# A two-layer graph network on one core: edges and stored products in transfers for two spans, one table for x1 and x1 @ W1m, degrees summed in layer 1, and four slots in the ring

## The chip, the cores and the metric

The kernel runs on 1 core of one Trainium2 chip. The metric is the device time of one execution in microseconds (us), and a version's time is the median of its runs. All engines (TensorE, VectorE, ScalarE, GpSimd, and SyncE, which here only issues transfers) work from instruction queues of their own. In the profile they are called PE (with PEld for its weight loads), DVE, ACT, POOL and SP.

## The reference

There are N = 6250 nodes with D = 256 features, and E = 106250 edges, sorted by their target `dst`, with 256 features each. Everything is float32. Both layers gather a row for each edge's source, and sum over the edges of each target:

```python
# layer 0
msg = relu(x[src] + edge_attr)
h   = 2 * x + segment_sum(msg, dst)
f   = gelu(bn1(h) @ W1.T + b1) @ W2.T + b2
x1  = layernorm(x + bn2(h + f))
# layer 1
m   = gelu((x1[src] + edge_attr) @ W1m + b1m) @ W2m + b2m
agg = segment_sum(m, dst) / maximum(deg, 1)          # deg: edges per target
u   = gelu(agg @ W1u + b1u) @ W2u + b2u
x2  = layernorm(x1 + layernorm(x1 + u))
```

The layer norms have no scale of their own except the inner one of layer 1.

## The kernel before

**Tiles, spans, blocks.** The edges lie in 831 tiles of 128. Eight tiles make a span (V = 104 spans), in two groups of four. The nodes lie in 25 blocks of 256 (the last has 106). Since the edges are sorted by target, the targets of a span fall in a short window of nodes.

**The ring.** The gathered rows of a span stand in one of `RING` = 5 buffers, `rings[v % RING]`. `gather` (L793) issues eight indirect DMAs on POOL for a span, each of 128 rows of 1 KB, and before the first of them POOL waits until span v - 5 has been read out of that buffer.

**Layer 0, a loop over spans** (`step_0`). In step v: SP loads the edges of span v + 3 (`load_edges`, L776, 1 MB); POOL gathers for v; PE transposes the edges of v's first group (`turned`, L806; ACT copies to eaT, L811) and multiplies them by W1m (`product`, L819), DVE copies that to the tile z (L1101, L1110), and SP stores z into `zst` (L1111, 512 KB), so that layer 1 need not multiply the first group again. For span v - 1 ACT copies the edges into PSUM (`lifted`, L830) and DVE adds them to the gathered rows (`add_to_gathered`, L837); ACT applies relu (`activated`, L845). For span v - 2 PE sums the rows into 128 slots by one-hot matrices (L854 makes them on DVE; `into_slots`, L876), and ACT copies the slots out of PSUM (`kept_slots`, L885). For span v - 3 PE sums the slots into the accumulators of the blocks (`into_blocks`, L904). The ring's rows have a column of ones behind the 256 features, so with a width of 257 the slots hold their number of edges as well; a further matmul (L912) and additions on DVE (L917) make the degree of each node, on one partition.

**Blocks of layer 0.** When a block has all of its edges, the generator `nodes_0` goes through its dense part, a stage in each step: it stores the degrees (L974, 1 KB), computes x1 and stores it to `x1d` (L1018), then y = x1 @ W1m + b1m, and stores that to `proj` (L1042).

**Layer 1** (`step_1`) has the same steps. It gathers from `proj`, takes the first group's product from `zst` (L1249, 512 KB), loads the second group's edges (L776, 512 KB) and multiplies them, and applies gelu. For each new block SP loads x1 (L1242) and the degrees, spread over all partitions (L1244). At the end of a step `invert()` (L1266 to L1268) computes max(deg, 1), its reciprocal, and min(deg, 1). `nodes_1` begins with the product of the sums and the reciprocal (L1174) and ends with the store of the output (L1233). The first gather of layer 1 waits for the last store into `proj`.

**Order.** All of this stands in `tc.manual_schedule()`: each engine's instructions run in the order in which the program writes them. In that order SP's loads for span v + 3 come at the beginning of step v, and the stages of the blocks come once in the middle of a step (`advance(early)`) and once at its end (`advance(late)`). `end_0` and `end_1` write out the last spans of a layer, and `finish` the stages that are left.

## Time and profile before

| what | us |
|---|---|
| median of 3 runs (2175.54 to 2177.23) | 2176.7 |
| the profiled execution | 2862.04 |
| its span | 2860.2 |
| busy in it: PE | 2061.7 |
| busy in it: POOL | 1577.4 |
| busy in it: DVE | 1404.1 |
| busy in it: ACT | 1344.0 |

The profile is of one execution, and that one took nearly a third longer than the runs of the median. Durations of single instructions are to be taken from it with that in mind, and its waits even more so. A row of a group gives its line, engine, operation, the tiles that it writes and reads, and the number of instructions; behind the bar stand its busy time, the mean of one in ns, the idle time of the engine just before them, and what ended most of that.

### The profile page before, as it was taken

The numbers are of one execution on the slowest core, as the hardware profiler recorded it, in microseconds if no ns is written. First come the engines' busy times: TensorE is split into PE (matmuls) and PEld (weight loads), VectorE is DVE, ScalarE is ACT, GpSimd is POOL, SyncE is SP. The second block draws the span as 40 slices with busy tenths as digits, with TensorE's granted clock in tenths as the row PEclk, the third lists the DMA queues.
The fourth block names the chain that finished last, engine by engine and source line by source line (L and its number), as shares of the span: only waits on it lengthen the run. The fifth ranks groups of instructions, "written<-read, shape, count | busy, mean of one in ns | idle before, by whom it ended". The sixth has DMA issues, their size and how long they took to land.

```text
span 2860.2 us, 37166 instructions
## 1 busy us (share of the span) xinstructions
PE 2061.7 (72%) x11784; PEld 1524.6 (53%) x11784; DVE 1404.1 (49%) x4130; ACT 1344.0 (47%) x2138; POOL 1577.4 (55%) x1671
## 2 busy tenths in 40 slices
PE   3688788878788788788357757766776666665876
PEld 2465556556566555556245545544555555554654
DVE  3455555455455555555134534454454445454545
ACT  1355555455555555555133534444444444443544
POOL 5566566565565566662555554555555554555550
PEclk7789999899899999999678888897888888887988
DMA  6667676676677676674545544554555554554540
GB/s 213 202 221 229 216 239 222 209 239 218 214 231 228 212 246 223 220 241 133 168 152 164 171 155 148 176 170 150 167 174 172 164 166 148 164 174 146 183 154 14
DMA packets 312069, 531.71 MB, mean 186 GB/s; under 512 B 36325, under 2 KB 231480, under 8 KB 311736
## 3 DMA queue, kind: packets, MB, share of 16 engines
q1 hardware_dynamic: 231416, 309.65, 32.2%
q0 software_dynamic: 79744, 217.71, 24.9%
q8 instruction: 97, 1.59, 0.2%
q10 hardware_dynamic: 704, 1.87, 0.2%
q14 instruction: 108, 0.88, 0.1%
HBM read 455.34 MB, written 73.75 MB: 185 GB/s over the span
## 4 chain that ended last, share of the span: by engine, by line
PE 22%; another core or an unknown queue 13%; DVE 6%; issue 5%; ACT 5%; DMA 1%; POOL 1%; ACTq 0%; DVEq 0%; POOLq 0%
PE workP L819 10%; PE acc L904 3%; PE slotP L876 3%; PE nodeP L1211 2%; PE workP L806 2%; DVE ring L837 1%; PE nodeP L1184 1%; DMA ring<-proj,src_sb 1%; DVE hot L854 1%; ACT L961 1%; ACT ring L845 1%; ACT workP L830 1%; ACT eaT L811 1%; DVE uT L1189 1%
## 5 line engine op out<-in xcount | busy, mean ns | idle before, releaser
L793 POOL DMA_INDIRECT ring<-proj,src_sb x831 | 788.1, 948 | 683.9 <-issue 362.3
L793 POOL DMA_INDIRECT ring<-in_x_dram,src_sb x831 | 787.5, 948 | 525.9 <-issue 246.3
L819 PE MATMUL workP<-w1m_sb,eaT 128*128 128x256 f32 x3324 | 910.1, 419 | 159.7 <-ACT eaT L811 113.0
L819 PEld LDWEIGHTS workP<-w1m_sb,eaT 128*128 128x128 f32 x3324 | 662.9, 208 | 369.0 <-ACT eaT L811 118.5
L837 DVE TENSOR_TENSOR ring<-workP,ring 128x512 f32<-128x512 f32 x832 | 542.2, 682 | 626.9 <-remote 381.5
L904 PE MATMUL acc<-hot,sums 128*128 128x160 f32 (+19 forms) x1360 | 264.2, 331 | 304.9 <-DVE hot L898 176.1
L845 ACT ACTIVATE ring<-ring 128x1024 f32<-128x1024 f32 x418 | 441.8, 1058 | 65.6 <-DVE ring L837 46.0
L830 ACT COPY workP<-ea 128x512 f32<-128x512 f32 x624 | 345.4, 596 | 121.2 <-DVE ring L837 76.2
L904 PEld LDWEIGHTS acc<-hot,sums 128*128 128x128 f32 x1360 | 209.6, 216 | 343.8 <-DVE hot L898 131.4
L885 ACT COPY sums<-slotP 128x257 f32<-128x257 f32 (+1 forms) x208 | 77.0, 370 | 631.6 <-remote 314.7
L811 ACT COPY eaT<-workP 128x512 f32<-128x512 f32 x416 | 227.0, 586 | 306.7 <-PE workP L806 179.3
L876 PE MATMUL slotP<-ring,hot 128*32 128x257 f32 (+1 forms) x3324 | 277.0, 416 | 121.5 <-remote 64.4
L806 PE MATMUL workP<-ident,ea 128*128 128x128 f32 x1662 | 252.1, 289 | 147.2 <-DVE z L1101 75.3
L806 PEld LDWEIGHTS workP<-ident,ea 128*128 128x128 f32 x1662 | 201.9, 148 | 213.6 <-DVE z L1101 97.0
L854 DVE TENSOR_SCALAR hot<-ramp,slot 128x32 f32<-128x32 f32 x1662 | 265.5, 257 | 0.0
L876 PEld LDWEIGHTS slotP<-ring,hot 128*32 128x32 f32 x3324 | 112.4, 115 | 251.5 <-issue 110.3
L1194 ACT ACTIVATE uT<-uT,cols_sb 128x256 f32<-128x256 f32 (+1 forms) x100 | 44.6, 495 | 257.6 <-DVE uT L1189 221.4
L917 DVE TENSOR_TENSOR degs<-degs,slotP 1x160 f32<-1x160 f32 (+24 forms) x170 | 36.3, 241 | 253.7 <-remote 104.8
L1101 DVE COPY z<-workP 128x512 f32<-128x512 f32 x104 | 71.1, 684 | 172.9 <-remote 104.7
L1184 PE MATMUL nodeP<-fT,w 128*128 128x256 f32 x368 | 92.8, 394 | 17.2 <-issue 16.1
L1110 DVE COPY z<-workP 128x512 f32<-128x512 f32 x104 | 71.3, 686 | 39.7 <-PE workP L819 26.2
L961 ACT ACT_TABLE_LOAD x70 | 89.8, 1283 | 1.2
(138 smaller groups left out, 1469.1 us busy)
## 6 DMA issues: line engine op xcount, KB each, us to landing
ea<-in_edge_attr_dram SPq DMA_DIRECT2D x103, 1024.0 KB
zst<-z SPq DMA_DIRECT2D x104, 512.0 KB
ea<-zst SPq DMA_DIRECT2D x104, 512.0 KB
ea<-in_edge_attr_dram SPq DMA_DIRECT2D x103, 512.0 KB
ring<-in_x_dram,src_sb POOLq DMA_INDIRECT x831
ring<-proj,src_sb POOLq DMA_INDIRECT x831
xb<-in_x_dram SPq DMA_DIRECT2D x24, 256.0 KB
x1d<-x SPq DMA_DIRECT2D x24, 256.0 KB
```

Of the source, the lines that this page charges most:

```text
L793: nc.gpsimd.indirect_dma_start(out=rings[v % RING][:n, g * G + j, :D], out_offset=None, in_=table, in_offset=bass.IndirectOffsetOnAxis(ap= ...
L806: nc.tensor.transpose(pe[:, j, k, :n], ea[:n, q + j, k * P : (k + 1) * P], ident[:n, :n])
L811: nc.scalar.copy(eaT[:, j:k, :, :n], pe[:, j:k, :, :n])
L819: nc.tensor.matmul(ph[:n, j, :], lhsT=eaT[:, j, k, :n], rhs=w1m_sb[:, k, :], start=(k == 0), stop=(k == KC - 1),)
L830: nc.scalar.copy(ps[:n, j:k, :], of[:n, q + j : q + k, :])
L837: nc.vector.tensor_add(r[:n, at + j : at + k, :D], ps[:n, j:k, :], r[:n, at + j : at + k, :D])
L845: nc.scalar.activation(at, at, func)
L854: nc.vector.tensor_scalar(hots[v][:n, j, :], ramp[:n, :SLOTS], slot[:n, t : t + 1], None, op0=ALU.is_equal,)
L876: nc.tensor.matmul(ps[q * SLOTS : (q + 1) * SLOTS, :width], lhsT=hot[:n, j, :], rhs=r[:n, j, :width], start=(i == 0), stop=(i == PAIR - 1 ...
L904: nc.tensor.matmul(acc[b][:, k, cols], lhsT=its[:, k * P : (k + 1) * P], rhs=at, start=(begins and k == 0), stop=(last_span[b] == v and k ...
L961: nc.scalar.activation(mv[:n, :H, 1], mv[:n, :H, 1], AF.Sqrt, bias=eps[:n, :])
L1184: nc.tensor.matmul(ps[:, o - i, :width], lhsT=w12[:, k, o * P : (o + 1) * P], rhs=mT[:, k, :width], start=(k == 0), stop=(k == KC - 1),)
```

## The change

The edges are loaded into tiles for two spans (three buffers of 16 KB per partition): 2 MB in one transfer in layer 0, and in layer 1 1 MB from `zst` and twice 512 KB of edges. z is one tile for two spans, in one buffer, and is stored once in two steps. x1 and y are written into one tile and stored together into `table`, [N, 2, 256]; layer 1 gathers rows of 1 KB from it with doubled indices (`twice_src`, made once on DVE), and loads x1 from every second row. The degrees are no longer summed in layer 0: layer 1 takes the slots with a width of 257, ACT spreads their counts over 128 columns (`counts`), and the matmul and the additions then give the degree of each node on all partitions. What `invert()` did stands at the beginning of `nodes_1`. The ring has four buffers. The diff, without the last spans' lines and renamed tiles of the setup:

```diff
 SPAN = P // SLOTS * PAIR
-RING = 5
+RING = 4
 ROW = 260
...
     dram = ctx.enter_context(tc.tile_pool(name="dram", bufs=1, space=bass.MemoryType.DRAM))
-    proj = dram.tile([N, D], F32, name="proj")
-    x1d = dram.tile([N, D], F32, name="x1d")
-    degd = dram.tile([1, N], F32, name="degd")
-    zst = dram.tile([len(window), P, G * D], F32, name="zst")
+    table = dram.tile([N, 2, D], F32, name="table")
+    x1d = table[:, 1, :]
+    pairs_of_spans = -(-len(window) // 2)
+    zst = dram.tile([pairs_of_spans, P, 2 * G * D], F32, name="zst")
...
         tc.tile_pool(name="state", bufs=1) as state,
-        tc.tile_pool(name="edges", bufs=AHEAD + 1) as ep,
+        tc.tile_pool(name="edges", bufs=3) as ep,
         tc.tile_pool(name="hots", bufs=2) as hp,
...
+        twice_src = check.tile([P, T], I32, name="twice_src")
+        def rows_of_table():
+            nc.vector.tensor_scalar(twice_src, src_sb, 2.0, None, op0=ALU.mult)
         def norms():
...
-        def load_edges(v, some, to):
-            counts = sum((tiles_of(v, g) for g in some), [])
+        eas = {}
+        def load_rows(to, t0, tiles):
+            counts = [min(P, E - t * P) for t in range(t0, min(T, t0 + tiles))]
             for j, k, n in runs(counts):
-                r0 = (v * SPAN + some[0] * G + j) * P
+                r0 = (t0 + j) * P
                 nc.sync.dma_start(
...
-        def edge_tiles(v):
-            ea = ep.tile([P, SPAN, D], F32, name="ea")
-            for g in range(GROUPS):
-                eas[v, g] = ea[:, g * G : (g + 1) * G, :]
-            return ea
-        def gather(v, table):
+        def edges_0(i, pieces=1):
+            if i >= pairs_of_spans:
+                return
+            ea = ep.tile([P, 2 * SPAN, D], F32, name="ea")
+            for h in range(2 * GROUPS):
+                eas[2 * i + h // GROUPS, h % GROUPS] = ea[:, h * G : (h + 1) * G, :]
+            m = 2 * SPAN // pieces
+            for h in range(0, 2 * SPAN, m):
+                load_rows(ea[:, h : h + m, :], 2 * i * SPAN + h, m)
+        def edges_1(i):
+            if i >= pairs_of_spans:
+                return
+            ea = ep.tile([P, 2 * SPAN, D], F32, name="ea")
+            spans = [v for v in (2 * i, 2 * i + 1) if v < V]
+            for h, v in enumerate(spans):
+                eas[v, 0] = ea[:, h * G : (h + 1) * G, :]
+                eas[v, 1] = ea[:, (h + GROUPS) * G : (h + GROUPS + 1) * G, :]
+            m = len(spans) * G
+            nc.sync.dma_start(
+                out=ea[:, :m, :].rearrange("p j d -> p (j d)"), in_=zst[i][:, : m * D]
+            )
+            for v in spans:
+                load_rows(eas[v, 1], v * SPAN + G, G)
+        def gather(v, of, rows):
             for g in range(GROUPS):
...
                         out_offset=None,
-                        in_=table,
-                        in_offset=bass.IndirectOffsetOnAxis(ap=src_sb[:n, t : t + 1], axis=0),
+                        in_=of,
+                        in_offset=bass.IndirectOffsetOnAxis(ap=rows[:n, t : t + 1], axis=0),
                     )
...
-        hots, hot2s, sums = {}, {}, {}
+        hots, hot2s, sums, counts = {}, {}, {}, {}
...
                     )
-            sums[v] = hp.tile([P, D + 1], F32, name="sums"), ps
+            sums[v] = hp.tile([P, D], F32, name="sums"), ps
             return ps[:, :width]
...
         def kept_slots(v, ps):
-            nc.scalar.copy(sums[v][0][:, : ps.shape[-1]], ps)
+            nc.scalar.copy(sums[v][0], ps[:, :D])
+            if ps.shape[-1] > D:
+                counts[v] = hp.tile([P, P], F32, name="counts")
+                nc.scalar.copy(counts[v], ps[:, D : D + 1].to_broadcast([P, P]))
...
             (its, ps), hot, lo0 = sums.pop(v), hot2s.pop(v), window[v][0]
-            rest = ps[:1, D + 1 :]
+            rest = ps[:, D + 1 :]
             for b, lo, hi in parts(v):
...
                 nc.tensor.matmul(
-                    rest[:, :span], lhsT=its[:, D : D + 1], rhs=hot[:, :span], start=True, stop=True
+                    rest[:, :span], lhsT=counts.pop(v), rhs=hot[:, :span], start=True, stop=True
                 )
...
-        def nodes_0(b, acc, xb, deg):
+        def nodes_0(b, acc, xb):
             width, H, n = shape(b)
-            nc.sync.dma_start(out=degd[:, b * SB : b * SB + width], in_=deg[:, :width])
             fT = npool.tile([P, KC, SB], F32, name="fT")
...
                 )
-            hT = npool.tile([P, KC, SB], F32, name="hT", bufs=3)
+            hT = npool.tile([P, KC, SB], F32, name="hT")
             nc.vector.tensor_copy(hT[:, :, :width], acc[:, :, :width])
...
             ps = node_work()
-            gT = npool.tile([P, KC, SB], F32, name="gT")
+            gT = npool.tile([P, 2 * KC, SB], F32, name="uT")
             for o in range(KC):
...
             nc.vector.tensor_add(ps, ps, xb[:n, :H, :])
-            x1 = npool.tile([P, SH, D], F32, name="x1")
+            both = npool.tile([P, SH, 2, D], F32, name="both", bufs=3)
+            y, x1 = both[:, :, 0, :], both[:, :, 1, :]
             nc.vector.tensor_add(x1[:n, :H, :], ps, bn2_b[:n, None, :].to_broadcast([n, H, D]))
...
             scaled(x1, x1, mv, n, H)
-            nc.sync.dma_start(out=rows_of(x1d, b), in_=x1[:n, :H, :])
             yield
...
             yield
-            y = npool.tile([P, SH, D], F32, name="y", bufs=3)
             ps = node_work()
...
             )
-            nc.sync.dma_start(out=rows_of(proj, b), in_=y[:n, :H, :])
-        eas, xbs, acc, degs = {}, {}, {}, {}
+            nc.sync.dma_start(
+                out=rows_of(table.rearrange("n a d -> n (a d)"), b),
+                in_=both[:n, :H].rearrange("p h a d -> p h (a d)"),
+            )
+        xbs, acc, zs = {}, {}, {}
         def load_0(v):
-            load_edges(v, range(GROUPS), edge_tiles(v))
             for b in range(blocks):
...
                     )
-            degs[b] = npool.tile([1, SB], F32, name="degs", bufs=4)
-            nc.vector.memset(degs[b], 0.0)
             return False
...
         def full_0(v):
-            for b in into_blocks(v, acc, opened_0, degs):
-                begun(b, nodes_0(b, acc.pop(b), xbs.pop(b), degs.pop(b)))
-        zs = {}
+            for b in into_blocks(v, acc, opened_0):
+                begun(b, nodes_0(b, acc.pop(b), xbs.pop(b)))
...
             if v < V:
-                gather(v, x)
+                gather(v, x, src_sb)
                 first = turned(v, 0, 0, eas[v, 0])
                 second = turned(v, 0, 2, eas[v, 0])
-                zs[v] = ep.tile([P, G, D], F32, name="z", bufs=2)
+                if v % 2 == 0:
+                    zs[v // 2] = ep.tile([P, 2, G, D], F32, name="z", bufs=1)
             if 0 <= u < V:
...
             if v < V:
-                nc.vector.tensor_copy(zs[v][:, 0:2, :], product(*first))
+                nc.vector.tensor_copy(zs[v // 2][:, v % 2, 0:2, :], product(*first))
             if 0 <= u < V:
...
                 activated(u, 0, AF.Relu)
+            if v % 2 == 0:
+                edges_0(v // 2 + 2)
             if 0 <= w < V:
                 slot_nodes(w)
-                kept_slots(w, into_slots(w, D + 1))
+                kept_slots(w, into_slots(w, D))
             if v < V:
-                nc.vector.tensor_copy(zs[v][:, 2:4, :], product(*second))
-                nc.sync.dma_start(out=zst[v], in_=zs.pop(v).rearrange("p j d -> p (j d)"))
+                nc.vector.tensor_copy(zs[v // 2][:, v % 2, 2:4, :], product(*second))
+                if v % 2 or v == V - 1:
+                    z, m = zs.pop(v // 2), v % 2 + 1
+                    nc.sync.dma_start(
+                        out=zst[v // 2][:, : m * G * D],
+                        in_=z[:, :m].rearrange("p s j d -> p (s j d)"),
+                    )
             advance(late)
...
             slot_nodes(u - 1)
-            kept_slots(u - 1, into_slots(u - 1, D + 1))
+            kept_slots(u - 1, into_slots(u - 1, D))
             advance(under_way)
...
             slot_nodes(u)
-            kept_slots(u, into_slots(u, D + 1))
+            kept_slots(u, into_slots(u, D))
             full_0(u)
...
                 load_1(v)
+            for i in range(2):
+                edges_1(i)
             finish()
...
-        def nodes_1(b, acc, x1, deg, inv):
+        def nodes_1(b, acc, x1, deg):
             width, H, n = shape(b)
+            inv = npool.tile([P, SB], F32, name="inv", bufs=1)
+            nc.vector.tensor_scalar(inv[:, :width], deg[:, :width], 1.0, None, op0=ALU.max)
+            nc.vector.reciprocal(inv[:, :width], inv[:, :width])
+            nc.vector.tensor_scalar(deg[:, :width], deg[:, :width], 1.0, None, op0=ALU.min)
             mT = npool.tile([P, KC, SB], F32, name="fT")
...
             yield
-            uT = npool.tile([P, UC, SB], F32, name="uT")
+            uT = npool.tile([P, max(UC, 2 * KC), SB], F32, name="uT")
             for i in range(0, UC, 2):
...
             nc.scalar.copy(ps[:n, :H, :], x1[:n, :H, :])
-            r = npool.tile([P, SH, D], F32, name="hT", bufs=3)
-            y = npool.tile([P, SH, D], F32, name="y", bufs=3)
+            both = npool.tile([P, SH, 2, D], F32, name="both", bufs=3)
+            r, y = both[:, :, 0, :], both[:, :, 1, :]
             for to, name in ((r, "L1_gnn_b2u"), (y, "L1_gnn_beta")):
...
-        x1s, degs_1, acc_1, invs = {}, {}, {}, {}
+        x1s, degs_1, acc_1 = {}, {}, {}
...
                     nc.sync.dma_start(out=x1s[b][:n, :H, :], in_=rows_of(x1d, b))
-                    degs_1[b] = npool.tile([P, SB], F32, name="degb", bufs=4)
-                    nc.sync.dma_start(
-                        out=degs_1[b][:, :width],
-                        in_=degd[:, b * SB : b * SB + width].to_broadcast([P, width]),
-                    )
-            edge_tiles(v)
-            nc.sync.dma_start(out=eas[v, 0].rearrange("p j d -> p (j d)"), in_=zst[v])
-            load_edges(v, [1], eas[v, 1])
...
             acc_1[b] = psa.tile([P, KC, SB], F32, name="acc")
-            fresh.append(b)
+            degs_1[b] = npool.tile([P, SB], F32, name="degs", bufs=4)
+            nc.vector.memset(degs_1[b], 0.0)
             return True
-        fresh = []
-        def invert():
-            while fresh:
-                b = fresh.pop()
-                width, deg = shape(b)[0], degs_1[b]
-                invs[b] = npool.tile([P, SB], F32, name="inv")
-                inv = invs[b][:, :width]
-                nc.vector.tensor_scalar(inv, deg[:, :width], 1.0, None, op0=ALU.max)
-                nc.vector.reciprocal(inv, inv)
-                nc.vector.tensor_scalar(deg[:, :width], deg[:, :width], 1.0, None, op0=ALU.min)
         def full_1(v):
-            for b in into_blocks(v, acc_1, opened_1):
-                begun(b, nodes_1(b, acc_1.pop(b), x1s.pop(b), degs_1.pop(b), invs.pop(b)))
+            for b in into_blocks(v, acc_1, opened_1, degs_1):
+                begun(b, nodes_1(b, acc_1.pop(b), x1s.pop(b), degs_1.pop(b)))
...
             if v < V:
-                gather(v, proj)
+                gather(v, table.rearrange("n a d -> (n a) d"), twice_src)
             some = 0 <= u < V
...
                 slot_nodes(w)
-                kept_slots(w, into_slots(w, D))
+                kept_slots(w, into_slots(w, D + 1))
+            if v % 2 == 0:
+                edges_1(v // 2 + 2)
             if some:
...
             advance(late)
-            invert()
...
         begin()
+        edges_0(0, pieces=2)
+        edges_0(1)
         for v in range(AHEAD):
             load_0(v)
...
-        beside = {1: norms, 2: weights_of_layer_1, 3: strays, 6: join_weights}
+        beside = {1: norms, 2: weights_of_layer_1, 3: strays, 4: rows_of_table, 6: join_weights}
```

More of the change, by code (lines that the diff above doesn't have):

```diff
@@ L657, in node_work @@
             return work() if draining else psn.tile([P, 2, D], F32, name="nodeP")
-        dst_sb = check.tile([P, T], I32)
+        dst_sb = check.tile([P, T], I32, name="edge")
         tiles_i = check.tile([P, T], I32)
@@ L724, in strays @@
         def strays():
-            off = check.tile([P, T], F32)
+            off = check.tile([P, T], F32, name="edge")
             nc.vector.tensor_copy(off, tiles_i)
@@ L1310, in end_1 @@
             full_1(u - 2)
-            invert()
             activated(u - 1, 1, AF.Gelu)
@@ L1316, in end_1 @@
             slot_nodes(u - 1)
-            kept_slots(u - 1, into_slots(u - 1, D))
+            kept_slots(u - 1, into_slots(u - 1, D + 1))
             advance(under_way)
@@ L1325, in end_1 @@
             slot_nodes(u)
-            kept_slots(u, into_slots(u, D))
+            kept_slots(u, into_slots(u, D + 1))
             full_1(u)
```

## The prediction

> **What bounds the kernel now.** I read the page first, then POOL's waits, then a stretch of the timeline in which POOL waits for nothing, then the chain of waits around the change of layers.
>
> ```profile
> span 2860.2 us, 37166 instructions
> PE 2061.7 (72%) x11784; PEld 1524.6 (53%) x11784; DVE 1404.1 (49%) x4130; ACT 1344.0 (47%) x2138; POOL 1577.4 (55%) x1671
> ...
> L793 POOL DMA_INDIRECT ring<-proj,src_sb x831 | 788.1, 948 | 683.9 <-issue 362.3
> L793 POOL DMA_INDIRECT ring<-in_x_dram,src_sb x831 | 787.5, 948 | 525.9 <-issue 246.3
> L819 PE MATMUL workP<-w1m_sb,eaT 128*128 128x256 f32 x3324 | 910.1, 419 | 159.7 <-ACT eaT L811 113.0
> ```
>
> The profiled execution took 2862.0 us (span 2860.2 and 1.8 around it), 685 us more than the median of 2176.7. Its shares of busy time are therefore not those of a timed run; what is wanted is the engine that would set 2176.7. The timeline shows the pace of the gathers when nothing holds them:
>
> ```profile
> 1379.09 0.98 POOL L793 DMA_INDIRECT ring<-proj,src_sb  x1 [63.28 <-DMA proj<-y]
> 1380.38 0.95 POOL L793 DMA_INDIRECT ring<-proj,src_sb  x1 [0.31 <-issue]
> ...
> 1390.38 0.95 POOL L793 DMA_INDIRECT ring<-proj,src_sb  x1 [0.30 <-issue]
> 1391.37 1.27 DVE L854 TENSOR_SCALAR hot<-ramp,slot 128x32 f32<-128x32 f32 x8
> 1391.64 0.94 POOL L793 DMA_INDIRECT ring<-proj,src_sb  x1 [0.30 <-DVE ring L837]
> 1392.88 0.95 POOL L793 DMA_INDIRECT ring<-proj,src_sb  x1 [0.30 <-issue]
> ```
>
> From start to start it is 1.25 us, though one is busy for 0.948: 1.25 is the cost. A span has 8 gathers, 10.0 us; a layer has 831, 1039 us. POOL's waits show where it loses time in the profile:
>
> ```profile
> POOL ring L793 <- issue: 608.6, 1265, 13.4
> POOL ring L793 <- ACT sums L885: 233.8, 94, 2.7
> ...
> POOL ring L793 <- DMA proj<-y: 63.3, 1, 63.3
> ```
>
> "sums L885" is kept_slots, the copy behind into_slots (L876), which is the last to read a slot of the ring: the gathers of span v wait for it in span v-5. Cut at the gathers, the profiled execution is 5.6 us to the first gather, 1310.2 of layer 0 (to 1315.8), 63.3 without a gather, 1408.7 of layer 1 (1379.1 to 2787.8), 72.4 to the end, and 1.8 around it: 2862.0. In the two layers 271 and 370 us are waits over 1.25 per gather. Without them 2221 remain. The sums into the last gathered rows of a layer come 25.1 and 23.6 us after its last gather, since the consumers trail in the profile; with gathers without a break they would trail by some 4 (the chain has 5.04 us from a gather to its sum), 41 us less: 2180, 0.15% from the median. So I take a timed run to be POOL's gathers end to end in both layers, with a bare chain at the change of layers (38 us from the last sums to the first gather) and at the end (49 us). PE is next, with 2061.7 us in all, 9.9 per span (modelled lengths, which run long when an input is late; I put it at 9.0). The windows give the clock and the shares by stage:
>
> ```profile
> 100.00:1300.00 1200.00, 971.05 (x5651) 707.00 (x5650) 627.70 (x1853) 635.00 (x1036) 723.11 (x764) 0.92 0.69 224
> 1300.00:1450.00 150.00, 75.63 (x419) 55.33 (x419) 49.91 (x152) 51.98 (x87) 55.75 (x59) 0.75 0.42 134
> ...
> 2800.00:2860.00 60.00, 36.60 (x183) 26.75 (x181) 31.41 (x96) 23.71 (x44) 0.00 (x0) 0.80 0.05 17
> ```
>
> The columns are PE, PEld, DVE, ACT and POOL busy, then the granted clock, the share of the DMA engines and GB/s.
>
> **The change part by part.**
>
> *Fewer and larger transfers.* In the two layers SP issues 52 stores of z less, 52 loads of zst, some 51 loads of edges, 25 stores (x1d and proj become one), 25 of degd and 25 of degb: about 230. No wait of POOL names one but the last proj store. The Trainium skill ("SBUF — State Buffer", The DMA setup-cost knee) gives a transfer a fixed cost of about 2 us and says to coalesce: 230 x 2 = 460 us by that rule, if they stood in a chain. By the rows they are issued three spans ahead of use by a queue that carries nothing else, so 0. I take 0; what covers them is POOL's 10 us per span, and without that cover the loads would still be ahead by 3.6 spans (2.6 before).
>
> *Four slots instead of five.* Gathers of span v+4 start 40 us after those of v at POOL's pace (50 before); by then into_slots(v) must be done. The rows of span v land by 10+3 us, its sums run a step behind, its slots a step behind that: some 22 to 28 us. 12 us are left, so 0 per span. At the start there is no such lead: the first sums wait for weights and edges (SP's first loads stand behind each other), and in the profile the gathers of span 5 start at 67.8 us after a wait of 12.3 for the first into_slots. A timed run without a break needs that by 55.6; with four slots it is needed by 45.6. Floor 0 (it is done by 45.6), ceiling 10 (it is done at 55.6 or later). If it falls anywhere from 35 to 55.6, the mean is 2.5 us; I take 2.5.
>
> *One z tile for two spans, one buffer.* The first copy of an even span (L1101) must wait for the landing of the store issued at the end of the odd step; two buffers covered it before. Behind it on DVE stand two sums and the second copy, and ACT and PE wait for those. The nearest row is the store of 512 KB: its last packet comes 3.7 us after the issue, so 1 MB about 6 (an estimate). Between the issue and the copy lie an early stage and the first two sums, 2 x 0.68 and the one-hots (8 x 0.16), so 1 to 3 us of DVE per two spans. DVE's busy time is 627.7 of layer 0's 1200 us; per span that is below 6.5 of 10 us. Hidden: 0, at most 3 x 52 = 156 us if consumers set the pace.
>
> *x1 and y in one table.* The gather reads 1 KB rows at a stride of 2 KB; each is still one packet of 1 KB: 0. The index table for it is one more DVE instruction of 831 elements at step 4; by L1266's 0.32 us for 256 elements about 1.0 (an estimate). The skill ("SBUF — State Buffer", the "DVE blocks DMA" trap) speaks against adding DVE work from SBUF to SBUF: it can keep POOL from writing descriptors. The timeline above has eight such instructions (L854, 1.27 us) across a gather, and the gathers stay 1.25 apart. By the rule +1.0, by the row 0: I take 0. The chain says what the table costs at the change of layers:
>
> ```profile
> 1367.15 5.28 PE workP L1034 x12
> 1372.90 5.26 DMA proj<-y
> 1378.37 0.52 issue
> ```
>
> The last store (106 rows) is on that path, and its rows become 2 KB. Packets of 1 KB take 46 ns, of 2 KB 84 by the trace. The skill ("DMA: Bandwidth & Descriptors", Why a DMA increments its semaphore by 16) says that the number of engines divides the number of rows: 2 for 106, so 53 x 38 ns = +2.0 us; spread over 16 engines +0.3. No row names the engines, but 5.26 us for 106 KB, longer than the 3.7 for 512 KB, speaks for two: +2.0.
>
> *Degrees.* Out of layer 0 go a matmul (L912, two entries of 0.32 us) and 1.6 sums (L917) per span:
>
> ```profile
> L1267 DVE RECIPROCAL inv<-inv 128x256 f32<-128x256 f32 (+1 forms) x25 | 42.9, 1716 | 0.9
> ...
> L917 DVE TENSOR_TENSOR degs<-degs,slotP 1x160 f32<-1x160 f32 (+24 forms) x170 | 36.3, 241 | 253.7 <-remote 104.8 <-issue 75.7 <-PE workP L819 37.6
> ...
> L1266 DVE TENSOR_SCALAR inv<-degb 128x256 f32<-128x256 f32 (+1 forms) x25 | 8.0, 320 | 0.0
> L1268 DVE TENSOR_SCALAR degb<-degb 128x256 f32<-128x256 f32 (+1 forms) x25 | 5.7, 226 | 0.0
> ```
>
> Into layer 1 come one more ACT copy per span (0.25 to 0.37, from 0.37 for L885) and the same matmul and sums. In either layer it lies under POOL's 10 us. At the change of layers L912 (0.63) and a sum (0.24) go for each of the last two spans, 1.7 at most; part of it stood beside ACT and DVE work: -1.0. At the end it is the reverse. Before, invert() ran when a block was opened; now max, reciprocal and min (0.32 + 1.72 + 0.23 = 2.27 us) stand at the head of nodes_1, after the last accumulation and the degree sums, ahead of the product that L1174 makes. The last two blocks are both in the closing chain: 2.27 for block 23, 1.1 for the 106 wide block 24 (its reciprocal took 0.82), and copy, matmul and sum 0.3 + 0.63 + 0.24. Floor 1.5 (most hidden behind PE's work on the other block), ceiling 6; I take 4.5, all but the matmul.
>
> Sum: start 2.5, change of layers +2.0 - 1.0, end +4.5: +8.0 us on 2176.7, 2184.7; against the profiled execution +8 as well, plus what a shorter ring adds to its waits.
>
> **The rivals.**
>
> *Not slower: transfers do hold POOL back.* The two chains of 38 and 49 us are the profile's, at a clock of 0.75 and 0.80; at full clock their PE parts (some 40 us) would be 9 us shorter, and without the pieces called "issue" (some 14) 23 in all. Then up to 23 us of 2176.7 are waits of POOL that I do not see. They would be gathers behind SP's packets on the same DMA engines (busy 69% in layer 0) or behind the landing of the gather eight before. Point: a landing over 10 us after issue; those that I looked at take 2.5 to 5.8, which speaks against it. With 230 transfers less and 8 us added elsewhere: 2177 - 23 + 8 = 2162.
>
> *The consumers, not POOL, decide once the ring is four.* If kept_slots(v) comes L us after the first gather of v, a span costs L/4 where it is over 10. L is at most 50 now. From 40 on each us costs 0.25 x 208 = 52 us: at 41, 2237. The profile has such an L (12.3 x 5 = 61), but its trailing is of that execution; my count is 22 to 28. The z wait would add to L.
>
> *It makes no difference:* kept_slots in time at the start and the closing work under PE: 2178.
>
> **How the numbers follow.** About 0.2% (4.4 us) is what a measurement of this kernel can tell from no change. POOL decides throughout, 0.49 (the third rival is its lower end): slower 0.37, within 0.2% 0.11, faster 0.01. Transfers hold POOL back, 0.37: faster 0.35, within 0.2% 0.02. Consumers decide, 0.14, all slower. Faster 0.36, same 0.13, slower 0.51. The likeliest case alone is 2178 to 2195; the range takes in most of the two others: 2148 to 2230.
>
> **What would show it.** Right: gathers 1.25 apart in both layers; from the last gather's sums to the first of layer 1 about 39 us, and to the end about 53; no wait of POOL on a transfer but the table store. The start: the wait ahead of span 4's gathers, longer by up to 10 us than the 12.3 before span 5's. Wrong: a wait of DVE's L1101 copies for zst of more than 3 us that the PE follows, or layer 0 shorter than 1039 us could be by gathers at 1.25 (then 1.25 is not the price), or a timed run above 2200 (four slots are too few).

## The result: slower by 0.5%, and the profile after

The changed kernel takes 2186.9 us (median of 5 runs, 2186.06 to 2188.2) against 2176.7 before; the ratio is 1.0047, with a 95% interval from 1.0032 to 1.0062. The forecast was 2184.7, in a likeliest case of 2178 to 2195. A second set of runs on another chip gave 2191.0 against 2182.6, a ratio of 1.0045 (1.0032 to 1.0059).

The profiled execution of the changed kernel ran at the speed of its timed runs (span 2186.1). From its page, the span, the busy time and the two groups of gathers (busy, mean ns | idle before, and what ended most of it):

```profile
span 2186.1 us, 36642 instructions
...
PE 1850.5 (85%) x11784; PEld 1458.9 (67%) x11784; DVE 1418.9 (65%) x4130; ACT 1353.5 (62%) x2242; POOL 1580.3 (72%) x1671
...
L822 POOL DMA_INDIRECT ring<-table,twice_src x831 | 789.0, 949 | 296.8 <-issue 146.5
L822 POOL DMA_INDIRECT ring<-in_x_dram,src_sb x831 | 789.5, 950 | 256.8 <-issue 148.3
```

Then what POOL waited for (total us, times, longest us):

```profile
POOL ring L822 <- issue: 294.9, 967, 0.6
POOL ring L822 <- DMA xb<-table: 44.0, 1, 44.0
POOL ring L822 <- DMA ring<-in_x_dram,src_sb: 30.2, 99, 0.3
```

The hundreds of us of waits that stood before POOL in the first profile are gone. What is left is a gap of 0.3 us per gather, a few short waits and one wait of 44.0 us. The gathers do run end to end, 1.25 us from start to start, through both layers, as the prediction took it for the timed runs. So most of the 10 us are to be found where POOL has nothing to issue, at the ends of the layers. To see them I also needed the kernel before at its timed speed, which is the first experiment.

### The profile page after: what moved, and what is told of

Read it like the earlier page. It is cut to its first block, busy times and chain, and to the rows that moved or that the text cites. A ratio compares the mean times of both kernels' runs of the same rounds, so it can differ in the third digit from the quotient of the medians.

```text
span 2186.1 us, 36642 instructions
## 1 busy us (share of the span) xinstructions
PE 1850.5 (85%) x11784; PEld 1458.9 (67%) x11784; DVE 1418.9 (65%) x4130; ACT 1353.5 (62%) x2242; POOL 1580.3 (72%) x1671
## 4 chain that ended last, share of the span: by engine, by line
PE 37%; DMA 28%; DVE 14%; issue 9%; ACT 7%; POOL 4%; DVEq 0%; ACTq 0%; POOLq 0%; SPq 0%
PE workP L848 16%; DMA ring<-in_x_dram,src_sb 14%; DMA ring<-table,twice_src 12%; POOL ring L822 4%; PE acc L936 4%; PE slotP L905 4%; DVE ring L866 4%; PE workP L835 3%; PE nodeP L1226 3%; ACT ring L874 2%; ACT workP L859 2%; DVE hot L883 2%; PE nodeP L1019 1%; DMA zst<-z 1%; PE nodeP L1253 1%
## 5 line engine op out<-in xcount | busy, mean ns | idle before, releaser
L822 POOL DMA_INDIRECT ring<-table,twice_src x831 | 789.0, 949 | 296.8 <-issue 146.5
L848 PE MATMUL workP<-w1m_sb,eaT 128*128 128x256 f32 x3324 | 850.1, 401 | 81.2 <-DVE ring L866 66.4
L866 DVE TENSOR_TENSOR ring<-workP,ring 128x512 f32<-128x512 f32 x832 | 554.4, 685 | 513.0 <-DMA ring<-in_x_dram,src_sb 175.6
L848 PEld LDWEIGHTS workP<-w1m_sb,eaT 128*128 128x128 f32 x3324 | 631.1, 198 | 251.2 <-issue 64.6
L936 PE MATMUL acc<-hot,sums 128*128 128x160 f32 (+19 forms) x1360 | 233.9, 306 | 147.1 <-DVE hot L892 86.2
L835 PE MATMUL workP<-ident,ea 128*128 128x128 f32 x1662 | 228.6, 280 | 40.4 <-DVE z L1130 16.9
L905 PE MATMUL slotP<-ring,hot 128*32 128x256 f32 (+1 forms) x3324 | 231.1, 389 | 13.1 <-DVE degs L949 7.2
L914 ACT COPY sums<-slotP 128x256 f32<-128x256 f32 x208 | 75.0, 361 | 87.2 <-PE slotP L905 86.9
L1130 DVE COPY z<-workP 128x512 f32<-128x512 f32 x104 | 70.8, 681 | 52.7 <-DMA zst<-z 38.0
L1226 PEld LDWEIGHTS nodeP<-fT,w 128*128 128x128 f32 x368 | 69.4, 193 | 31.9 <-DVE both L1267 23.2
L1253 PE MATMUL nodeP<-w2u_sb,uT 128*128 128x256 f32 x352 | 83.1, 391 | 0.0
```

The costliest lines, as they stand in the source:

```text
L822: nc.gpsimd.indirect_dma_start(out=rings[v % RING][:n, g * G + j, :D], out_offset=None, in_=of, in_offset=bass.IndirectOffsetOnAxis(ap=row ...
L835: nc.tensor.transpose(pe[:, j, k, :n], ea[:n, q + j, k * P : (k + 1) * P], ident[:n, :n])
L848: nc.tensor.matmul(ph[:n, j, :], lhsT=eaT[:, j, k, :n], rhs=w1m_sb[:, k, :], start=(k == 0), stop=(k == KC - 1),)
L866: nc.vector.tensor_add(r[:n, at + j : at + k, :D], ps[:n, j:k, :], r[:n, at + j : at + k, :D])
L905: nc.tensor.matmul(ps[q * SLOTS : (q + 1) * SLOTS, :width], lhsT=hot[:n, j, :], rhs=r[:n, j, :width], start=(i == 0), stop=(i == PAIR - 1 ...
L936: nc.tensor.matmul(acc[b][:, k, cols], lhsT=its[:, k * P : (k + 1) * P], rhs=at, start=(begins and k == 0), stop=(last_span[b] == v and k ...
```

## The experiments

**The kernel before again (e1), with four slots alone (e2), and the changed kernel with the degrees as before (e3).**

> The kernel before, unchanged, for a profile at its timed speed (the first profile of it took 2862 us). Theory (POOL's gathers end to end, the loss at the two ends of the layers): span near 2175, gathers 1.25 apart in both layers (each about 1039 us from the first to the last), about 43 us from the last gather of layer 0 to the first of layer 1 (44.0 in the changed kernel), and about 47 us from the last gather to the end (51.5 in the changed kernel). Rival (the gathers themselves are slower in the changed kernel, held by four slots or by transfers): both gaps as in the changed kernel within 1 us, and the layers some 5 us shorter each.

Measured: 2179.5 us (ratio to the kernel before 1.0006, 0.9997 to 1.0014), span 2178.8. POOL's waits at this speed (total us, times, longest us), in place of the 608.6 and 233.8 of the first profile:

```profile
POOL ring L793 <- issue: 298.6, 980, 0.3
POOL ring L793 <- DMA proj<-y: 39.2, 1, 39.2
```

So the kernel before is POOL's gathers end to end as well. With both kernels at timed speed, the trace can be cut at the same instructions. The columns are us; "waits" is what a layer's gathers take over 1.251 each; the gap and the closing part run from the end of a layer's last gather.

| | first gather | layer 0 (waits) | gap to layer 1 | layer 1 (waits) | closing part | span |
|---|---|---|---|---|---|---|
| before (e1) | 6.0 | 1041.5 (2.3) | 39.2 | 1042.1 (2.9) | 50.0 | 2178.8 |
| four slots alone (e2) | 5.7 | 1042.3 (3.1) | 37.7 | 1041.5 (2.3) | 48.8 | 2175.9 |
| changed | 5.4 | 1043.3 (4.1) | 44.0 | 1041.8 (2.6) | 51.5 | 2186.1 |
| changed, again (g1) | 5.7 | 1043.2 (4.0) | 44.1 | 1042.6 (3.4) | 49.5 | 2185.2 |
| degrees as before (e3) | 5.6 | 1042.4 (3.2) | 42.4 | 1041.3 (2.1) | 47.1 | 2178.8 |

The gap was expected at 43 us and is 39.2; the closing part was expected at 47 and is 50.0. The rival, layers 5 us shorter and equal gaps, falls. The first and third rows differ by 7.3 us: 4.9 in the gap, 1.5 at the close, 1.8 in layer 0, and -0.9 in the two other columns. The two executions of the same changed kernel differ by 2 us in the closing part, so a difference of 2 us between two single profiles proves nothing by itself.

The gap splits into three pieces: from the last gather to the last sum, from there to the last store, and from the store to layer 1's first gather. Before they are 1.8, 31.2 and 6.2 us; changed 6.0, 29.6 and 8.5. The chain of waits shows the pieces. Before (e1; start, duration, what):

```profile
1045.41 2.70 DMA ring<-in_x_dram,src_sb
...
1074.82 5.22 PE workP L1034 x12
...
1080.51 5.26 DMA proj<-y
```

and changed:

```profile
1046.59 6.92 DMA ring<-in_x_dram,src_sb
...
1078.94 4.86 PE workP L1064 x12
...
1084.58 8.00 DMA xb<-table
```

The last row in each is the landing of the last store (the time until its last data have arrived), for which the first gather of layer 1 waits (in the changed kernel the view names the load issued just behind it). The first row is new: the last gathers of layer 0 land late. What SP does at that moment (start, us of issuing, transfer):

```profile
1046.10 0.32 SPq L1144 DMA_DIRECT2D zst<-z  x1
...
1046.47 0.43 SPq L1284 DMA_DIRECT2D xb<-table  x1
...
1047.00 2.28 SPq L812 DMA_DIRECT2D ea<-zst  x1
...
1049.32 1.17 SPq L784 DMA_DIRECT2D ea<-in_edge_attr_dram  x2
...
1050.60 1.12 SPq L812 DMA_DIRECT2D ea<-zst  x1
1051.76 2.93 SPq L784 DMA_DIRECT2D ea<-in_edge_attr_dram  x2
1053.63 1.04 DVE L866 TENSOR_TENSOR ring<-workP,ring 128x512 f32<-128x512 f32 x2 [5.35 <-DMA ring<-in_x_dram,src_sb]
```

In the changed kernel nothing holds SP there, and 4 MB for layer 1 go out around the last gather (its end is at 1048.7). In the kernel before, SP stands at the stores of the degrees until 1059 and only then loads for layer 1 (e1):

```profile
1042.54 0.32 SPq L1111 DMA_DIRECT2D zst<-z  x1
...
1052.55 6.59 SPq L974 DMA_DIRECT2D degd<-degs  x2
...
1060.49 0.36 SPq L1249 DMA_DIRECT2D ea<-zst  x1
```

The trace's packets (the single rows of a transfer) agree: from 5 us before to 10 us after the last gather SP's queue starts 3.8 MB in the changed kernel and 0.8 before, and the last packet of the gathers ends 5.1 us after the last gather, against 1.0.

e2 is one line:

```diff
-RING = 5
+RING = 4
```

> The kernel before with four slots in the ring and nothing else changed. Theory (the ring costs only at the start, where span 4's gathers would wait for the first into_slots): 0 to 3 us over the kernel before, 2177 to 2180. Rival (the ring is what costs the 10 us): 2185 to 2188, with waits of POOL all along layer 0.

Measured: 2177.5 us, ratio 0.9997 (0.9989 to 1.0006). In the kernel before, four slots cost nothing that can be measured. With five slots the changed kernel (e4) does not fit into the on-chip memory, so it has no time, and the ring is judged from e2. In the changed kernel POOL waits 0.8 us for a slot, once, ahead of the seventh span; e2 has no wait there, and f4 below comes back to it.

e3 undoes the degrees part:

```diff
-            nc.scalar.copy(sums[v][0], ps[:, :D])
-            if ps.shape[-1] > D:
-                counts[v] = hp.tile([P, P], F32, name="counts")
-                nc.scalar.copy(counts[v], ps[:, D : D + 1].to_broadcast([P, P]))
+            nc.scalar.copy(sums[v][0][:, : ps.shape[-1]], ps)
...
+            nc.sync.dma_start(out=degd[:, b * SB : b * SB + width], in_=deg[:, :width])
...
+                    nc.sync.dma_start(
+                        out=degs_1[b][:, :width],
+                        in_=degd[:, b * SB : b * SB + width].to_broadcast([P, width]),
+                    )
...
-            inv = npool.tile([P, SB], F32, name="inv", bufs=1)
...
+            invert()
```

> The changed kernel with the degrees as before: summed in layer 0 on one partition, stored and loaded again, invert() at the end of a step. Theory (max, reciprocal and min stand on the closing chain): the time from the last gather to the end falls by 3 to 5 us, the change of layers gains about 1; 2182 to 2185 in all. Rival (ring, z tile or transfers cost all): 2186 to 2188, the closing time unchanged at 51 to 52.

Measured: 2181.8 us, ratio 1.0018 (1.0009 to 1.0028): the changed kernel stood 8.5 to 10.2 us over the kernel before, so about half of it goes. In the profiles the closing part falls from 51.5 and 49.5 to 47.1, and the gap from 44.0 to 42.4. The closing part of the changed kernel on DVE (start, us, what; in brackets the idle time before):

```profile
2139.58 0.37 DVE L949 TENSOR_TENSOR degs<-degs,slotP 128x50 f32<-128x50 f32 x2
2139.87 0.28 DVE L1212 TENSOR_SCALAR inv<-degs 128x256 f32<-128x256 f32 x1
2140.19 1.75 DVE L1213 RECIPROCAL inv<-inv 128x256 f32<-128x256 f32 x1
2141.86 0.23 DVE L1214 TENSOR_SCALAR degs<-degs 128x256 f32<-128x256 f32 x1
2142.00 0.68 DVE L1216 TENSOR_TENSOR fT<-acc,inv 128x512 f32<-128x512 f32 x1
2142.59 1.00 DVE L866 TENSOR_TENSOR ring<-workP,ring 128x512 f32<-128x512 f32 x2
```

and of e3:

```profile
2132.99 1.29 DVE L1243 TENSOR_TENSOR both<-nodeP,rows_sb 128x512 f32<-128x512 f32 x2 [2.19 <-ACT nodeP L1239]
2134.19 0.68 DVE L1213 TENSOR_TENSOR fT<-acc,inv 128x512 f32<-128x512 f32 x1
2134.79 1.00 DVE L867 TENSOR_TENSOR ring<-workP,ring 128x512 f32<-128x512 f32 x2
```

In the changed kernel 2.4 us (2139.58 to 2142.00) of degree sums, max, reciprocal and min stand ahead of the product, and the last sums of the whole program (L866) stand behind both. In e3 the product follows the work before it directly. The gain in the gap agrees with the picture above: in e3 the stores of the degrees hold SP back again (the layer-1 loads leave at 1062, not at 1047), and the last packet of the gathers ends 1.7 us after the last gather. But there the store of z leaves earlier too, 3.0 us ahead of the last gather instead of 1.7, so e3 does not tell the two apart.

**The parts at the change of layers, and the z tile (f1, f2, f4), and fewer gathers (f3).** On the chip of this set the kernel before took 2831 us (2807 to 2854 in eleven runs), and the profiles of the set have waits of POOL as in the first profile, so ratios are to be taken within the set alone.

f1 delays the first layer-1 loads:

```diff
-            for i in range(2):
-                edges_1(i)
-            finish()
+            left = len(running)
+            while len(running) == left:
+                advance(list(running))
+            edges_1(0)
+            finish()
+            edges_1(1)
```

> The changed kernel, in which the first layer-1 transfers (zst and edges of four spans) leave SP later: two spans' behind the first table store of the closing part of layer 0, two spans' behind the last. Theory (at the change of layers these 4 MB go out at the moment of layer 0's last gathers, and their landing takes 6.9 us instead of 2.7): the last sum comes 1 to 2 us after the last gather instead of 5.5, the time without a gather falls from 44.0 to about 40, and the whole to about 2183. Rival (the last gathers land late for another reason, or what is won there is lost by the loads later): 44 us and 2186 to 2188.

Measured: 2779.9, against 2831.3 before (0.9783, 0.9718 to 0.9848). Here the last sum comes 17.6 us after the last gather, since the consumers are that far behind, so the landing decides nothing, and the run can't speak to either side. The edit stands in g2 again.

f2 cuts the last block's table store:

```diff
+            whole = n if n == P else n // 16 * 16
+            for lo, hi in ((0, whole), (whole, n)):
+                if lo < hi:
...
+                    nc.sync.dma_start(
+                        out=rows[lo:hi], in_=both[lo:hi, :H].rearrange("p h a d -> p h (a d)")
+                    )
```

> The changed kernel with the table store of the last block (106 rows) cut into two, of 96 and of 10 rows. Theory (106 rows are carried by two of the 16 engines, and their 2 KB packets make the landing 8.0 us): the first gather of layer 1 starts about 5.5 us after the last store instead of 8.3; 2184 in all. Rival (the landing is late because the store of the block before, now 512 KB, stands ahead of it in the same queue): unchanged, 8 us and 2187.

Measured: 2788.3 (0.9825, 0.9771 to 0.988). The total is again that of this chip, but the piece in question has its own row in the timeline, SP's stores and POOL's next gather:

```profile
1401.04 1.75 SPq L1076 DMA_DIRECT2D table<-both  x3
...
1405.73 0.98 POOL L822 DMA_INDIRECT ring<-table,twice_src  x1 [49.37 <-DMA xb<-table]
```

The 96-row store starts at 1401.83, so the first gather follows in 3.9 us (5.5 was expected). With 106 rows of 2 KB in one store it took 8.2 to 8.9 in all six profiles of such kernels, and with 106 rows of 1 KB 6.2 to 6.3 in all five. The rival, the 512 KB store ahead, falls: that store is there in f2 as well. The trace's packets show the mechanism itself: in the changed kernel the 2 KB packets of the uncut store run two at a time from 1087.3 to 1091.4 us, while those of the store ahead of it ran 16 at a time; with the cut (j below) about 16 run at a time through both stores, until 1085.0.

f4 stores z for each span again:

```diff
-                if v % 2 == 0:
-                    zs[v // 2] = ep.tile([P, 2, G, D], F32, name="z", bufs=1)
+                zs[v] = ep.tile([P, G, D], F32, name="z", bufs=2)
...
```

> The changed kernel with z as before: a tile for each span in two buffers, stored by itself (512 KB), into the paired zst. Theory (the wait of DVE's z copies for the landing, 38 us in all in the changed kernel's profile, is hidden under POOL's gathers): the wait goes, the time stays at 2186 to 2188. Rival (the single z tile costs in layer 0): 2177 to 2183.

Measured: 2792.2 (0.9877, 0.9827 to 0.9927). It is no faster than f1 and f2, so nothing speaks for the rival, but at this chip's speed the run does not show a cost or its absence at 2187. The changed kernel's profile has the wait, and it is on an engine that is 65% busy (DVE, total us, times, longest):

```profile
DVE z L1130 <- DMA zst<-z: 38.0, 21, 8.9
```

The longest of these waits is not quite hidden. From the chain of waits of the changed kernel, and POOL's gather behind it:

```profile
26.50 16.45 DMA zst<-z
...
43.05 0.70 DVE z L1130
...
66.98 1.00 PE slotP L905 x16
```

```profile
68.30 0.94 POOL L822 DMA_INDIRECT ring<-in_x_dram,src_sb  x1 [1.07 <-ACT ring L874]
```

The first store of z lands 16.45 us after its issue, the copy waits 8.9 us for it, PE follows, and the chain goes on, through 7 us of one-time DVE work (L728 to L736), to the sums that free the slot for the seventh span: this is POOL's wait of 0.8 us. It stands at the same gather in all five profiles with transfers for two spans at about 2180 us (0.5 to 1.9 us) and in none of e1, e2 and g4. After the twenty other waits (up to 4.1 us) no wait of POOL inside layer 0 is longer than 0.6 us.

f3 leaves gathers out of the kernel before (their rows are set to zero once at the start):

```diff
...
+                    if j == 3:
+                        continue
```

> The kernel before without the gathers of every fourth tile (six of eight in a span; those rows keep what the ring holds). Theory (POOL's gathers set the time of both layers): the span takes what the next engine needs, PE at about 9.0 us; 1950 to 2010 in all. POOL alone would give 7.5 per span and 1660. Rival (the consumers set the time already): over 2150.

Measured: 2197.2, against 2831.3. That is in the rival's range, but on a chip on which the kernel before takes 2831. A quarter fewer gathers took 634 us away, more than their issue costs (414 gathers x 1.25 = 518), so more than POOL's issue is lost on this chip. The granted clock was 0.95 in the runs of f3 and 0.86 to 0.88 in all others of the set; whether that is a cause or a consequence, no run here settled. f1, f2 and f4 are 1.2 to 2.2% faster than the kernel before on it, and which part of the change does that stays open too.

**The same questions on a chip on which the kernel before takes 2182.6 us (g1 to g4).** g1 is the changed kernel itself:

> The changed kernel itself once more, beside the three others of this set. Theory (POOL's gathers end to end, with the loss at the change of layers and at the end): 8 to 11 us over the kernel before where that takes about 2177. Where the kernel before takes about 2830, as on the chip of the second set, its gathers wait for the consumers; there the changed kernel should be faster by 1 to 2%, as its variants were.

Measured: 2191.0, ratio 1.0045, as quoted at the top; its cuts are in the table. g2 is f1 again:

> The late layer-1 transfers of f1 again, on this chip. Theory: where the changed kernel takes about 2187, the last sum of layer 0 comes 1 to 2 us after the last gather instead of 5.5, and the whole is 3 to 4 us shorter than the changed kernel. Rival: no difference, the time without a gather stays 44.

Measured: 2190.8, ratio 1.0043 (1.0029 to 1.0057): no difference from g1. The profile shows that what was to happen did happen, in part: the last gather packet ends 2.9 us after the last gather (g1 4.5), the last sum ends at 4.5 (g1 5.7), and the gap is 42.6 instead of 44.1. But 1.5 us of gap are less than two executions differ by elsewhere (here 2.2 us more of small waits in layer 0, 1.9 in layer 1). So the collision with the layer-1 loads is seen in the trace, but no run shows that it costs time, and it is the smaller part of the late landing: with the loads out of the way the last sum still comes 4.5 us after the last gather, in e1 1.8. The 1 MB store of z also leaves at that moment (1046.10 above), where the kernel before stores 512 KB, and earlier. The profile of j, below, speaks for that store.

g3 is f3 again:

> The kernel before with six of eight gathers in a span, again (every fourth tile's rows are left as the ring holds them). In the second set it took 2197, with PE at 9.85 us per span in layer 0. Theory (POOL sets the time of the kernel before, PE is close behind it): where the kernel before takes about 2177, this one takes 2000 to 2100. Rival (PE sets the time already, and POOL only looks busy): 2165 to 2200.

Measured: 1939.1, ratio 0.8891 (0.8877 to 0.8904). That is below the expected 2000 to 2100 and far from the rival. It settles what sets the kernel before: with a quarter fewer gathers it is 243 us faster. The windows inside the layers (busy PE, PEld, DVE, ACT, POOL, then granted clock, share of the DMA engines, GB/s) and POOL's waits:

```profile
100.00:850.00 750.00, 746.24 (x5096) 580.17 (x5095) 578.50 (x1678) 569.59 (x943) 492.65 (x520) 1.00 0.89 295
1000.00:1800.00 800.00, 735.21 (x4845) 580.28 (x4837) 590.93 (x1739) 550.10 (x848) 526.76 (x555) 1.00 0.71 227
```

```profile
POOL ring L797 <- issue: 358.0, 722, 5.2
...
POOL ring L797 <- ACT ring L849: 53.6, 29, 4.5
POOL ring L797 <- ACT workP L834: 42.0, 57, 5.6
```

Now POOL waits again and PE is at 99 and 92%. A span takes 8.6 us (layer 0's 897 us over 104 spans), 1.4 us under POOL's 10.0. In layer 0 that is PE's pace; which consumer sets it in layer 1, with PE at 92%, is not shown.

g4 carries f2's cut to the kernel before, for the last block's stores into proj and into the output:

```diff
+            whole = n // 16 * 16
+            nc.sync.dma_start(out=rows_of(to, b)[:whole], in_=y[:whole, :H, :])
+            if whole < n:
+                nc.sync.dma_start(out=rows_of(to, b)[whole:], in_=y[whole:n, :H, :])
```

> The kernel before, with the last block's stores into proj and into the output cut into 96 and 10 rows. Theory (106 rows go through two of the 16 engines; in the changed kernel the cut took 4.5 us from the time between the last store and the first gather of layer 1): 6.2 us from that store to the first gather become about 4, and the last store lands 2 us sooner; 4 us less than the kernel before, about 2173. Rival (the last store's landing is hidden or is not bound by its engines): no change.

Measured: 2176.5 against 2182.6, ratio 0.9977 (0.9968 to 0.9985). SP's stores (the first row holds the block before and the 96 rows) and POOL's first gather of layer 1:

```profile
1080.63 1.27 SPq L976 DMA_DIRECT2D proj<-y  x2
1081.95 0.36 SPq L978 DMA_DIRECT2D proj<-y  x1
...
1084.46 0.98 POOL L793 DMA_INDIRECT ring<-proj,src_sb  x1 [35.47 <-PE workP L819]
```

From the 96-row store (1081.58) to the gather it is 2.9 us, where it was 6.2. At the end, from the last store to the end of the span, it is 5.5 where it was 7.5. The 6.0 us are more than the 4 expected. Of the kernels with all gathers, on the chips where the kernel before takes 2177 to 2183 us, it is the fastest against the kernel before of its own set.

**The change with its costly parts mended (j).** It joins the edits of e3, f1 and f2, and cuts the output store as in g4.

> The changed kernel with three of its parts mended at once: degrees as before (e3), the first layer-1 transfers late (g2), and the last block's stores into the table and into the output cut into 96 and 10 rows (f2, g4); paired edges and z, the table and four slots stay. Theory (what the change costs stands at the two ends and is the sum of these): e3 stood 4.0 us over the kernel before; the cut takes 4.4 at the change of layers and 2 at the end; 2 to 4 us less than the kernel before, ratio 0.998 to 0.999. Rival (the paired transfers and four slots cost something inside the layers too): 1 to 4 us more than the kernel before.

Measured: 2176.1 against 2177.7, ratio 0.9991 (0.9983 to 1.0). Its gap is 38.4 us, its closing part 44.5. It lies between the two expectations and nearer to the first: the sum of the mended parts covers what the change cost, to within a few us. But the fair comparison is g4, the kernel before with the same cut (0.9977, up to 0.9985): transfers for two spans, the table and four slots bring nothing, and may still cost up to 3 us. In the traces the gap is 38.4 us against 35.5 in g4: 1.0 of it is the 2 KB rows (3.9 us from the 96-row store to the first gather, against 2.9), and 2.8 the landing of the last gathers (the last sum 4.8 us after the last gather, against 2.0). From the chain of waits and SP's transfers in j:

```profile
1047.67 5.16 DMA ring<-in_x_dram,src_sb
```

```profile
1047.26 0.33 SPq L1148 DMA_DIRECT2D zst<-z  x1
```

Between 1033 and 1055 us that store of 1 MB is the only transfer that SP issues, and the loads for layer 1 leave at 1069. So they are not needed for a late landing. The likeliest cause is the store of z, which leaves 0.4 us ahead of the last gather; no run at this speed changes that store alone, so that is not shown.

## Why the prediction was right, point by point

- **The bound.** Right. The timed runs are POOL's gathers end to end; the profiles of e1 and of the changed kernel show it, and g3 proves it. PE's pace was put at 9.0 us per span, and g3 has 8.6.
- **Fewer and larger transfers: 0.** Right. 230 transfers less moved neither layer by more than 2 us (first to last gather 1041.5 and 1042.1 before, 1043.3 and 1041.8 changed), nowhere near the 460 that the prediction reckoned for a chain.
- **Four slots: 0 inside the layers, 2.5 at the start.** The first is right. The start was mis-sized: e2 shows no cost. I had taken the late first into_slots from the first profile, where the gathers behind it stood at 67.8 us.
- **One z tile: 0.** Right in the result, though the sign that was named for being wrong did appear: waits of more than 3 us of DVE's copies for zst, 8.9 and 4.1, the first with PE behind it. The first reached POOL, for 0.8 us. And where POOL does not cover it, at the end of layer 0, the 1 MB store is the likeliest cause of the late landing; the prediction had put nothing at either place.
- **The change of layers: +2.0 - 1.0.** The store's term was right, in size and in mechanism: from store to first gather 6.2 us became 8.2 to 8.9, its packets go two at a time, and the cut into 96 and 10 rows made it 3.9. The degrees' term of -1.0 can't be told from the spread: from the last sum to the last store it is 31.2 us in e1 and 29.6 in the changed kernel, but 29.7 in e2, which has the degrees as before, and 29.3 to 29.7 in g1 and g2. What the sum lacked altogether was the piece before it: the last gathers' landing, +4.2 us from the last gather to the last sum. I had costed transfers by their number and by POOL's cover inside the layers, and not asked what meets the last gathers: the store of z, now 1 MB, and the 4 MB of layer-1 loads that the stores of the degrees had held back on SP. The gap grew by 4.9 us in place of 1.0; in g2 moving the loads wins back 1.5 of it, and most of the late landing is still there in j.
- **The end: +4.5.** The mechanism was right: the reciprocal and its neighbours stand on the closing chain, 2.4 us in one piece. Undoing the degrees (e3) takes 2.4 to 4.4 us from the closing part. Against the kernel before, the closing part grew by only 1.5, and in g1 it shrank by 0.5, in part because the two kernels do not run their last products at the same granted clock. From 5 us before the end of the last gather to 3 us after it (e1, then e3; the clock is the third number from the end):

```profile
2123.79:2131.79 8.00, 6.31 (x31) 4.20 (x32) 4.14 (x16) 3.41 (x7) 3.81 (x4) 0.57 0.25 71
```

```profile
2126.70:2134.70 8.00, 6.03 (x44) 3.83 (x44) 5.22 (x16) 4.55 (x9) 3.79 (x5) 1.00 0.25 71
```

  It is 0.57 in e1 and e2 and 0.79 in g4, but 1.00 in all five profiles with transfers for two spans, and 11 products of the last span (L819) take 4.6 us in e1 and 2.5 in e3 and the changed kernel. So about 2 us (4.6 - 2.5) of what the degrees cost was paid back by something that the prediction did not have; why the clock differs there, no run settled.
- **The sum.** +8.0 was forecast; +10.2 and +8.5 were measured. The terms at the start and the end were too high together by about as much as the landing was missing. So the bound, the sign and where the cost lies were reasoned, but that the sum came within 2.2 us is luck: its parts are off by 2.5 to 5 us and cancel.
- **The rivals.** Transfers that hold POOL back, 2162: no. A POOL wait on a transfer inside a layer is at most 0.3 us long, and all waits inside the two layers of e1 come to 5.2 us, where this rival needed up to 23. Consumers decide with four slots, over 2200: no, by e2, and by POOL's waits inside the layers of the changed kernel, 6.7 us in all. No difference: no, though the interval begins at 0.3%.

## What to carry to other kernels

Find first the queue that is never idle. Here it is the one that issues the gathers, and then only what stands where that queue is empty costs anything: the start, the change of layers, the end. There, look at the last small transfer as closely as at a loop: two stores of 106 rows, each cut into 96 and 10, were worth more (6 us in g4) than 230 transfers inside the loops. And when a step is taken out of a queue, ask what it had been holding back, since the work behind it now starts at a different moment and meets something else.

## What the hardware did that was not expected

- A gather's issue does get longer beside some DVE work. Around 55 us in the changed kernel's profile:

```profile
53.61 0.99 POOL L822 DMA_INDIRECT ring<-in_x_dram,src_sb  x1 [0.30 <-issue]
53.90 0.58 DVE L728 CAST edge<-tiles_i 128x831 f32<-128x831 int32 x1
...
54.51 1.02 DVE L729 SCALAR_TENSOR_TENSOR edge<-edge,dstf 128x831 f32<-128x831 f32 x1
54.90 1.45 POOL L822 DMA_INDIRECT ring<-in_x_dram,src_sb  x1 [0.30 <-issue]
55.57 0.59 DVE L730 TENSOR_SCALAR edge<-edge 128x831 f32<-128x831 f32 x1
```

  Three gathers beside DVE instructions over 831 elements from SBUF to SBUF (L729 to L734) took 1.38 to 1.45 us instead of 0.95; beside `twice_src` (0.58 us) one took 1.16. But beside the cast of L728, of the same size, one took 0.99, and beside the reduction of L736 0.95, so length alone does not decide it. The rows of 32 elements that I had used as evidence show none of it. So the warning that the prediction weighed and put at 0 has something to it, at 0.2 to 0.5 us a gather beside some long instructions; which ones and why, no run settled. For this change it is 0.2 us in all, since the kernel before has L728 to L736 too.
- One store of 106 rows of 2 KB keeps the next layer waiting for 8.2 to 8.9 us, two of 96 and 10 rows for 3.9. For rows of 1 KB it is 6.2 and 2.9.
- The kernel before takes 2177 to 2183 us on the chips of the other sets and 2831 on that of f1 to f4, at a granted clock of 0.95 and 0.87. A quarter fewer gathers gave 1939 on one of the former and 2197 on the latter.
